# Lists one segment sooner, and GpSimd's fills, an ownership mask, a PSUM bank and a work slot moved, in a segmented attention kernel

## The chip, the cores and the metric

The kernel runs on 1 core of a Trainium2 chip. The metric is the device time of one execution in microseconds (us). Engines: PE (TensorE, matrix products), DVE (VectorE), ACT (ScalarE), POOL (GpSimd, which here also issues the indirect DMAs) and SP (SyncE, which issues most plain DMAs). The core has 16 DMA engines.

## What is computed

```python
N, d = feat.shape                       # 16384, 256; B = 8 segments, LMAX = 3072
q, k, v = feat @ Wq, feat @ Wk, feat @ Wv                       # q, k: 32 columns
starts = jnp.searchsorted(bids, jnp.arange(B)); pos = jnp.arange(N) - starts[bids]
pad = lambda x: jnp.zeros((B, LMAX, x.shape[-1])).at[bids, pos].set(x)
scores = where(mask[:, None, :], einsum('bld,bmd->blm', pad(q), pad(k)), NEG)
rp = einsum('blm,bmd->bld', softmax(scores), pad(v))
t = rp[bids, pos] @ Wt
tn = (t - t.mean(0)) / sqrt(t.var(0) + EPS) * gamma + beta
return feat + relu(tn)
```

The segment numbers `bids` come unsorted, so `pos` of most tokens falls outside 0 to LMAX - 1. Only the tokens that own a slot of a segment take part in its attention (up to 768 a segment on this path). All others read a segment's edge row or nothing.

## The kernel before

Everything is in one function, `fast_path`, which emits for each engine one in-order stream; a small scheduler (`Program`) places the waits. `Wv @ Wt` is folded into one matrix, `wvt`.

- **Lists.** For segment e, `owners(e)` makes the mask of its owners on DVE (seven instructions, up to the running count in `lm[:, e]`). `prefix(lo, hi)` sums counts over partitions by two small PE products into a PSUM bank, and DVE copies them out. `list_tests(e)` writes `ge`, two comparisons of `it16` with the counts, on DVE. `list_half(e, h, bank)` issues six small PE products of `ge` and `lm`; its `finish` turns them on DVE into `idx`, the tokens' numbers, and has GpSimd gather their rows of `feat` into `xs`, three tiles of 128 rows for each half. There are nine lists: 0 to 7 for the segments (up to six tiles), and list 8 (NB) for the repeated rows, tokens that lose their slot to another (up to three tiles, one half, gathered late into `xl` and `tl`).
- **Attention.** Segment e has up to six strips u of 128 query rows. For strip (e, u): `attend` sums PE products over the tiles into PSUM bank `ps_o[u % 2]`; `attended` has DVE take the reciprocal (`rdens`) and ACT write the scaled strip to `tk`, which frees the bank. Beside it the next segment is prepared: `xt_main`, `xt_rest` (turned rows), `project` (q, k), `values` (vs), `scores` (pa, pb). These share two banks `ps_m`, taken in turn by `nb()`; `ps_s[0..3]` hold the scores and, in between, list products. ACT's `square` and DVE's `moments` add up `acc`, the sums for mean and variance.
- **Slots.** Work not tied to a strip waits in a queue, `work`; `slot()` runs one piece of it on DVE: `everyone` (ownership of segments 4 to 7 and list 8), `third` (list 3's ownership, sums and tests), `tables` (row numbers), `one_hot` (matrices `hot`, from rows `eb` that SP loads). `steps` says at which strips of segments 0 to 3 a slot runs.
- **Order of the lists.** In the loop over e, list e + 2 is made at the start of segment e (list 7 in segment 5, list 8 in segment 6), and the tests of list e + 3 at strip 4 of segment e.
- **Fills.** GpSimd's `set` calls clear buffers: a first run at the start, and one behind the gathers of lists 0 and 1: `acc`, `xl`, `tl`, `ridl`, `ecat` and the 16 numbers `turn_of`.
- **The last stage.** After segment 7 the statistics give a scale and a shift. The 16 output groups of 1024 rows (1 MB each) are loaded from `feat` into nine buffers `fb` by `group_in(i)` on SP's queue, DVE or ACT adds the edge rows, and SP stores them. `rows(e)` normalizes the strips in `tk` on DVE, and GpSimd writes them to their rows by 41 indirect DMAs, each segment's behind the store of the last group that it touches. The first buffer `fb[0]` lies over `lm`, `ge`, `it16` and `pos`, so `group_in(0)` has to come behind the last list; it is called at strip (6, 1), and `group_in(1)` at (6, 3).

```python
        ahead = e + 2
        LTs = FT if ahead < NB else LT
        for u in range(FT):
            if ahead <= NB and u == 0 and e:
                first = list_half(ahead, 0, ps_s[2])
            attend(e, u)
            ...
            slot(int(u in steps.get(e, range(FT))))
            if u == 4 and e + 3 <= NB and e:
                list_tests(e + 3, FT if e + 3 < NB else LT)
```

Of the kernel before, what the change touches and what calls it, by code (L numbers as in the profile page):

```python
# [899 lines left out]
def fast_path(nc, feat, bids, wq, wk, wv, wt, gamma, beta, out, bad):  # L900
# [231 lines left out]
    pg.set("POOL", ones_n[:], 1.0 / N)  # L1132
    pg.set("POOL", rdens[:], 1.0)
    pg.set("POOL", graw[:], 0.0)
    for i in range(4):
        s = slice(32 * i, 32 * i + NB)
        pg.dma("SP", graw[s, 0, :], gamma.rearrange("(c i) -> c i", i=32))
        pg.dma("SP", graw[s, 1, :], beta.rearrange("(c i) -> c i", i=32))
# [311 lines left out]
    xt_rest(0, sB)  # L1450
    h1()
    last_()
    pg.set("POOL", acc[:], 0.0)
    pg.set("POOL", xl[:], 0.0)
    pg.set("POOL", tl[:], 0.0)
    pg.set("POOL", ridl[:], NB * FW)
    pg.set("POOL", ecat[:], 0.0)
    for i, g in enumerate(ORDER):
        pg.set("POOL", turn_of[:, g : g + 1], float(i + 1))
    values(0, 0, bank[1])  # L1460
    scores(0, 0, range(4))
    project(0, 1, ps_m[0])
# [22 lines left out]
    def everyone():  # L1485
        def a():
            pg.tt(m3[:], over_e(b_f[:]), over_j(ecol[:]), ALU.is_equal)

        def b():
            pg.tt(w3[:], m3[:], over_j(st_bc[:]), ALU.mult)  # L1490

        def c():
            by_token(pos[:], w3[:])
            pg.tt(pos[:], tok[:], pos[:], ALU.subtract)

        def d():
            pg.ts(below[:], pos[:], -float(LMAX), ALU.is_lt)
            pg.ts(above[:], pos[:], float(LMAX), ALU.is_ge)
            pg.ts(neg[:], pos[:], 0.0, ALU.is_lt)
            pg.tt(lose[:], neg[:], below[:], ALU.subtract)  # L1500
            pg.tt(lose[:], lose[:], same[:], ALU.mult)
            pg.tt(own[:], below[:], above[:], ALU.add)
            pg.tt(own[:], own[:], lose[:], ALU.add)
            pg.ts(own[:], own[:], -1.0, ALU.mult, 1.0, ALU.add)

        def f():
            pg.tt(o3[:], m3[:], over_e(own[:]), ALU.mult)
            for e in range(4, NB):
                pg.scan(lm[:, e, 0:J], ones[:], o3[:, e, :])
            pg.scan(lm[:, NB, 0:J], ones[:], lose[:])  # L1510

        def g():
            for go in prefix(4, NL, ps_s[3]):
                go()

        def g2():
            def by_e(x):
                return x.unsqueeze(2).to_broadcast([1, NB, NG])

            def by_g(x):  # L1520
                return x.unsqueeze(1).to_broadcast([1, NB, NG])

            pg.ts(g16[:], irow[0:1, 0:NG], float(GT * P), ALU.mult)
            pg.tt(gcmp[:], by_e(st_hi[0:1, :]), by_g(g16[:]), ALU.is_gt)
            pg.ts(g16[:], g16[:], float(GT * P), ALU.add)
            pg.tt(gcmp2[:], by_g(g16[:]), by_e(st_lo[0:1, :]), ALU.is_gt)
            pg.tt(gcmp[:], gcmp[:], gcmp2[:], ALU.mult)
            pg.tt(gcmp[:], gcmp[:], by_g(turn_of[:]), ALU.mult)
            pg.red(grp[:], gcmp[:], ALU.max)
            pg.ts(upto[:], grp[:], 1.0, ALU.max)  # L1530
            pg.red(lastg[:], grp[:], ALU.max)
            pg.ts(lastg[:], lastg[:], 1, ALU.max)
            pg.ts(third_l[:], n_bc[0:1, NB:NL], float((LT - 1) * P), ALU.is_gt)
            pg.copy("DVE", armf[:], tiles_i[:])
            pg.red(grp[:, 0:1], armf[:])
            pg.tt(grp[:, 0:1], grp[:, 0:1], third_l[:], ALU.add)
            pg.ts(writes[:], grp[:, 0:1], float(4 * NB + LT - 1), ALU.add, 16.0, ALU.mult)
            pg.ts(over[:, 0:NB], n_bc[:, 0:NB], float(FW), ALU.is_ge)
            pg.ts(over[:, NB:NL], n_bc[:, NB:NL], float(LW), ALU.is_ge)

        def h():
            pg.copy("DVE", br_f[:], br_i[:])
            pg.tt(reads[:], br_f[:], b_f[:], ALU.is_equal)
            pg.stt(reads[:], pos[:], 0.0, reads[:], ALU.is_ge, ALU.mult)
            pg.tt(reads[:], reads[:], own[:], ALU.add)
            pg.dma("SP", reads_of.rearrange("(p j) x -> p (j x)", j=J), reads[:])

        return [a, b, c, d, f, g, h, g2]
# [129 lines left out]
    reads_at = {(NB - 4, 2 + t): (NB - 2, (t,)) for t in range(4)}  # L1678
    reads_at.update({(NB - 3, t): (NB - 2, (3 + t,)) for t in (1, 2)})
    reads_at.update({(NB - 3, 3 + t): (NB - 1, (2 * t, 2 * t + 1)) for t in range(3)})  # L1680
    lag, ready = [], []
    steps = {0: (1, 2, 3, 4, 5), 1: (0, 1, 2, 4, 5), 2: (0, 2, 3, 5), 3: (0, 1, 2, 3, 5)}
    def third():
        owners(3)
        first, then, last_ = prefix(3, 4, ps_s[3])
        first()
        then()
        last_()
        list_tests(3, FT)
# [3 lines left out]
    for e in range(NB - 1):  # L1693
        n = e + 1
        for eng in ("PE", "ACT", "DVE"):
            pg.register(eng, n, tiles_i[0:1, n : n + 1], 2)
        if e == 1:
            todo, choose = tables()
            work.extend(todo)
        if e == 2:  # L1700
            work.extend(one_hot())
            work.append(choose)
        ahead = e + 2
        LTs = FT if ahead < NB else LT
        for u in range(FT):
            if ahead <= NB and u == 0 and e:
                first = list_half(ahead, 0, ps_s[2])
            attend(e, u)
            if e == 0 and u == 0:
                second_list()  # L1710
                attended(e, u)
                first = list_half(ahead, 0, ps_s[2])
            if ahead <= NB and u == 0:
                first()
                if LTs == FT:
                    second = list_half(ahead, 1, ps_s[3])
            slot(int(u in steps.get(e, range(FT))))
            if u == 4 and e + 3 <= NB and e:
                list_tests(e + 3, FT if e + 3 < NB else LT)
            if u == 4:  # L1720
                values(n, 0)
            if u == 5:
                values(n, 1)
            if e == NB - 2 and u == 3:
                group_in(1)
            if (e, u) != (0, 0):
                opened = attended(e, u)
            if u == 0:
                if ahead <= NB and LTs == FT:
                    second()  # L1730
                if ahead == NB:
                    others()
                xt_main(n, 0)
                xt_main(n, 1)
            if u == 1:
                xt_rest(n)
                project(n, 0)
                scores(e, 1, None)
            if u == 3:
                project(n, 1)  # L1740
                scores(n, 0, range(4))
            if u == 4:
                scores(n, 0, range(4, 6))
            if u == 5:
                values(n, 2)
            for x in ready:
                moments(*x)
            ready = []
            lag.append((e, u))
            for _ in range(0 if e == 0 else 2 if u % 2 else 1):  # L1750
                if lag:
                    square(*lag[0])
                    ready.append(lag.pop(0))
            if e == 0 and u == 1:
                pg.tr32(gb[:].rearrange("p s i -> p (s i)"), graw[:].rearrange("p s i -> p (s i)"))
                for e_ in range(3, NB):
                    pg.dma(
                        "SP", xs[:, e_ * FT : (e_ + 1) * FT, :], zt[:].unsqueeze(1).to_broadcast([P, FT, D]), [opened]
                    )
            if e == 0 and u in (1, 5):  # L1760
                pg.copy("ACT", spot[:], ones[:, 0:1])
            if (e, u) in reads_at:
                gather_reads(*reads_at[e, u], opened)
            if e == NB - 2 and u == 1:
                group_in(0)
            if e == NB - 2 and u > 3:
                group_in(u - 2)
            if e == NB - 2 and u == 5:
                group_in(4)
            if e == 4 and u == 3:  # L1770
                pg.set("POOL", tk[:, TT - 2 : TT, :], 0.0)
                pg.register("POOL", "writes", writes[:], 16 * (6 * NB + LT), 16 * (4 * NB + LT - 1))
                pg.register("POOL", "lastg", lastg[:], NG, 1)
                pg.register("POOL", "third", third_l[:], 1)
                for e_ in range(NB):
                    pg.register("POOL", ("g", e_), upto[0:1, e_ : e_ + 1], NG, 1)
                    pg.register("POOL", e_, tiles_i[0:1, e_ : e_ + 1], 2)
# [238 lines left out]
```

## Time and profile before

| | |
|---|---|
| time, median of 3 runs | 312.52 us (310.84 to 314.01) |
| the profiled execution's own time | 313.69 us, of which the span is 311.4 us |
| busy in the span | PE 252.2 us (81%), DVE 229.3 (74%), ACT 135.8 (44%), POOL 129.7 (42%) |
| DMA | 56.82 MB, mean 182 GB/s |
| chain that ended last | PE 39%, DVE 30%, DMA 14%, ACT 7%, issue 6%, POOL 2% |
| mean granted clock of PE | 0.906 |

In a row of a timeline stand the start in us, the duration, the engine, the source line (often that of a helper that records the operation), the operation, what it writes and reads, the shape, a count, and in square brackets how long the engine had been idle and what ended that. A fp32 product shows as two PE instructions.

### The profile page before, as it was taken

The numbers are of one execution on the slowest core, as the hardware profiler recorded it, in microseconds if no ns is written. First come the engines' busy times: TensorE is split into PE (matmuls) and PEld (weight loads), VectorE is DVE, ScalarE is ACT, GpSimd is POOL, SyncE is SP. The second block draws the span as 40 slices with busy tenths as digits, with TensorE's granted clock in tenths as the row PEclk, the third lists the DMA queues.
The fourth block names the chain that finished last, engine by engine and source line by source line (L and its number), as shares of the span: only waits on it lengthen the run. The fifth ranks groups of instructions, "written<-read, shape, count | busy, mean of one in ns | idle before, by whom it ended". The sixth has DMA issues, their size and how long they took to land.

```text
span 311.4 us, 4481 instructions
## 1 busy us (share of the span) xinstructions
PE 252.2 (81%) x1194; PEld 166.8 (54%) x1194; DVE 229.3 (74%) x718; ACT 135.8 (44%) x292; POOL 129.7 (42%) x155
## 2 busy tenths in 40 slices
PE   1779689899799898999999999989977786573820
PEld 1656555766575677687878778757523221121200
DVE  7866788779999896736664765767389999999600
ACT  7346234258474628644754583564421121211110
POOL 3436580340350071006312853742212347778674
PEclk9989796999999999999999999999998579859575
DMA  3102069422122021112021320579999999999984
GB/s 98 35 24 67 3 203 346 157 82 69 52 84 71 34 70 29 67 61 80 27 95 36 90 94 24 196 259 378 339 364 408 349 421 413 402 419 393 424 358 177
DMA packets 23240, 56.82 MB, mean 182 GB/s; under 512 B 4768, under 2 KB 15858, under 8 KB 19114
## 3 DMA queue, kind: packets, MB, share of 16 engines
q1 hardware_dynamic: 17434, 45.77, 39.2%
q0 software_dynamic: 5232, 10.18, 10.2%
q10 hardware_dynamic: 544, 0.52, 0.5%
q8 instruction: 13, 0.21, 0.3%
q14 instruction: 17, 0.14, 0.1%
HBM read 26.73 MB, written 28.61 MB: 178 GB/s over the span
## 4 chain that ended last, share of the span: by engine, by line
PE 39%; DVE 30%; DMA 14%; ACT 7%; issue 6%; POOL 2%; DVEq 1%; SPq 0%; POOLq 0%; ACTq 0%
PE ps L807 37%; DMA out<-f 14%; DVE acc L846 4%; DVE f L826 3%; DVE w L826 2%; DVE junk L833 2%; PE ps L812 2%; DVE k L823 2%; DVE tk L826 2%; POOL out L892 2%; ACT pa L817 1%; DVE ge L835 1%; ACT xT L817 1%; ACT tk L817 1%; DVE both L851 1%
## 5 line engine op out<-in xcount | busy, mean ns | idle before, releaser
L882 POOL DMA_INDIRECT xs<-in_r_feat,idx x48 | 51.0, 1063 | 101.2 <-DVE idx L846 77.1
L807 PE MATMUL ps<-vs,pa 128*128 128x257 f32 x312 | 73.6, 384 | 4.7 <-ACT sq L817 3.6
L807 PEld LDWEIGHTS ps<-vs,pa 128*128 128x128 f32 x312 | 57.1, 189 | 16.5 <-ACT sq L817 4.8
L807 PE MATMUL ps<-f,ident 128*128 128x512 f32 x52 | 38.3, 855 | 19.6 <-DMA f<-in_r_feat 14.4
L892 POOL DMA_INDIRECT out<-tk,idx x39 | 42.9, 1100 | 26.8 <-DVE tk L826 10.4
L817 ACT ACTIVATE tk<-ps,rdens 128x256 f32<-128x256 f32 x46 | 22.2, 483 | 61.8 <-DVE rdens L859 61.8
L807 PE MATMUL ps<-wvt,xT 128*128 128x256 f32 x156 | 39.6, 405 | 0.3 <-ACT pa L817 0.3
L822 ACT COPY f<-ps 128x512 f32<-128x512 f32 x26 | 13.9, 590 | 58.9 <-PE ps L807 58.9
L807 PEld LDWEIGHTS ps<-wvt,xT 128*128 128x128 f32 x156 | 30.9, 202 | 11.0 <-issue 4.3
L807 PEld LDWEIGHTS ps<-f,ident 128*128 128x128 f32 x52 | 11.7, 259 | 36.5 <-DMA f<-in_r_feat 19.3
L846 DVE SCALAR_TENSOR_TENSOR acc<-sq,reads_r,acc 128x256 f32<-128x256 f32 x45 | 21.6, 480 | 8.8 <-ACT sq L817 8.8
L817 ACT ACTIVATE pa<-ps,mask 128x512 f32<-128x512 f32 x39 | 24.0, 690 | 7.5 <-PE ps L807 7.4
L826 DVE TENSOR_TENSOR tk<-tk,ps 128x1024 f32<-128x1024 f32 (+1 forms) x30 | 24.2, 843 | 0.3
L882 POOL DMA_INDIRECT reads_r<-reads_of,idx x12 | 13.4, 1120 | 24.8 <-ACT sq L817 11.8
L826 DVE TENSOR_TENSOR f<-f,ps 128x512 f32<-128x512 f32 x38 | 23.3, 681 | 0.6 <-PE ps L807 0.6
L807 PE MATMUL ps<-q,k 32*128 32x512 f32 (+2 forms) x154 | 21.2, 486 | 1.5 <-ACT pa L817 1.1
L846 DVE SCALAR_TENSOR_TENSOR acc<-tk,reads_r,acc 128x256 f32<-128x256 f32 x45 | 21.5, 478 | 1.2 <-ACT tk L817 0.7
L807 PE MATMUL ps<-xT,w 128*128 128x512 f32 (+1 forms) x60 | 20.5, 474 | 0.5 <-ACT xT L817 0.4
L823 DVE COPY k<-ps 32x128 f32<-32x128 f32 x40 | 11.8, 294 | 12.0 <-PE ps L807 11.1
L807 PE MATMUL ps<-vs,pb 128*128 128x257 f32 x82 | 19.6, 387 | 0.0
L807 PEld LDWEIGHTS ps<-vs,pb 128*128 128x128 f32 x82 | 15.0, 189 | 6.5 <-issue 2.3
L817 ACT ACTIVATE q<-ps,cqk 96x512 f32<-96x512 f32 (+3 forms) x24 | 14.6, 608 | 7.3 <-PE ps L807 7.0
(260 smaller groups left out, 357.1 us busy)
## 6 DMA issues: line engine op xcount, KB each, us to landing
f<-in_r_feat SPq DMA_DIRECT2D x16, 1024.0 KB, 12.8
out<-f SPq DMA_DIRECT2D x16, 1024.0 KB, 15.8
t_rows<-tk SPq DMA_DIRECT2D x8, 512.0 KB, 3.9
xs<-zt SPq DMA_DIRECT2D x5, 768.0 KB, 10.3
t_rows<-tk SPq DMA_DIRECT2D x8, 256.0 KB, 2.2
eb<-edge_of SPq DMA_DIRECT2D x16, 96.0 KB, 2.3
xs<-in_r_feat,idx POOLq DMA_INDIRECT x48, 2.8
out<-tk,idx POOLq DMA_INDIRECT x39, 7.2
```

The costliest lines, as they stand in the source:

```text
L807: "PE", lambda e: e.matmul(out, lhsT, rhs, start=start, stop=stop, skip_group_check=True),
L812: return self.op("PE", lambda e: e.transpose(out, in_, ident), [in_, ident], [out])
L817: "ACT", lambda e: e.activation(out, in_, func, bias=bias, scale=scale), [in_, *more], [out]
L822: return self.op("ACT", lambda e: e.copy(out, in_), [in_], [out])
L823: return self.op(eng, lambda e: e.tensor_copy(out, in_), [in_], [out])
L826: return self.op(eng, lambda e: e.tensor_tensor(out, a, b, op), [a, b], [out])
L833: lambda e: e.tensor_scalar(out, a, s1, s2, op0, op1, accum_out=accum)
L835: else e.tensor_scalar(out, a, s1, s2, op0, op1),
L846: else e.scalar_tensor_tensor(out, a, s, b, op0, op1),
L851: return self.op("DVE", lambda e: e.tensor_reduce(out, in_, AX.X, op), [in_], [out])
L882: lambda e: e.indirect_dma_start(out=out, out_offset=None, in_=table, in_offset=bass.IndirectOffsetOnAxis(ap=ind, axis=0), bounds_check=n ...
L892: lambda e: e.indirect_dma_start(out=table, out_offset=bass.IndirectOffsetOnAxis(ap=ind, axis=0), in_=src, in_offset=None, bounds_check=n ...
```

## The change

- GpSimd's fill of `acc` goes to the first run of fills; the others, as `later_sets`, to the end of strip (1, 0), behind the gathers of list 3.
- `owners(3)` leaves `third` and is called in strip (0, 0), between the second list's tests and its halves.
- `prefix(4, NL)` takes a bank by `nb()` instead of `ps_s[3]`.
- The slot of strip (1, 5) runs behind `attended` instead of ahead of it.
- List 7 is made in segment 4: tests at strip 1, both halves at strip 2 in the `nb()` banks. List 8's tests go to strip 4 of segment 4, its half to the start of segment 5; `others()`, which uses it, stays in segment 6.
- `group_in(0)` is called at strip (5, 1).

```diff
@@ fills
     pg.set("POOL", graw[:], 0.0)
+    pg.set("POOL", acc[:], 0.0)
 ...
-    pg.set("POOL", acc[:], 0.0)
-    pg.set("POOL", xl[:], 0.0)
-    pg.set("POOL", tl[:], 0.0)
-    pg.set("POOL", ridl[:], NB * FW)
-    pg.set("POOL", ecat[:], 0.0)
-    for i, g in enumerate(ORDER):
-        pg.set("POOL", turn_of[:, g : g + 1], float(i + 1))
+    def later_sets():
+        pg.set("POOL", xl[:], 0.0)
        ...
@@ everyone, g
-            for go in prefix(4, NL, ps_s[3]):
+            for go in prefix(4, NL):
@@ the loop over the segments
+    LATE = ((1, 5),)
     def third():
-        owners(3)
 ...
-        ahead = e + 2
+        ahead = e + 2 if e < 5 else NB if e == 5 else NL
 ...
                 second_list()
                 attended(e, u)
+                owners(3)
                 first = list_half(ahead, 0, ps_s[2])
 ...
-            slot(int(u in steps.get(e, range(FT))))
-            if u == 4 and e + 3 <= NB and e:
-                list_tests(e + 3, FT if e + 3 < NB else LT)
+            if e == NB - 4 and u == 1:
+                list_tests(NB - 1, FT)
+            if e == NB - 4 and u == 2:
+                halves = [list_half(NB - 1, h, nb()) for h in range(2)]
+                for go in halves:
+                    go()
+            if (e, u) not in LATE:
+                slot(int(u in steps.get(e, range(FT))))
+            if u == 4 and e in (1, 2, 3, 4):
+                list_tests(e + 3 if e < 4 else NB, FT if e < 4 else LT)
 ...
                 opened = attended(e, u)
+            if (e, u) in LATE:
+                slot()
 ...
-                if ahead == NB:
+                if e == NB - 2:
                     others()
 ...
+            if e == 1 and u == 0:
+                later_sets()
 ...
-            if e == NB - 2 and u == 1:
+            if e == NB - 3 and u == 1:
                 group_in(0)
```

More of the change, by code (lines that the diff above doesn't have):

```diff
@@ L1452, in fast_path @@
     last_()
-    pg.set("POOL", acc[:], 0.0)
-    pg.set("POOL", xl[:], 0.0)
-    pg.set("POOL", tl[:], 0.0)
-    pg.set("POOL", ridl[:], NB * FW)
-    pg.set("POOL", ecat[:], 0.0)
-    for i, g in enumerate(ORDER):
-        pg.set("POOL", turn_of[:, g : g + 1], float(i + 1))
+    def later_sets():
+        pg.set("POOL", xl[:], 0.0)
+        pg.set("POOL", tl[:], 0.0)
+        pg.set("POOL", ridl[:], NB * FW)
+        pg.set("POOL", ecat[:], 0.0)
+        for i, g in enumerate(ORDER):
+            pg.set("POOL", turn_of[:, g : g + 1], float(i + 1))
     values(0, 0, bank[1])
```

## The prediction

> **What bounds the kernel now.** I read the page's slices first, to find the stages, then the table of windows, one row for each stage, then the timelines of the engines where an engine has holes.
>
> ```profile
> core 0: us, PE busy (x) PEld busy (x) DVE busy (x) ACT busy (x) POOL busy (x), PEclk, DMA share, GB/s
> 57.00:122.00 65.00, 59.02 (x316) 43.18 (x314) 58.53 (x200) 36.88 (x89) 19.24 (x18) 1.00 0.22 66
> 122.00:194.00 72.00, 71.14 (x392) 55.60 (x392) 42.93 (x145) 40.67 (x94) 25.06 (x23) 1.00 0.20 62
> 206.00:230.00 24.00, 20.53 (x75) 12.95 (x73) 13.76 (x46) 11.77 (x28) 5.60 (x6) 1.00 0.98 360
> 230.00:294.00 64.00, 43.15 (x165) 14.68 (x166) 62.05 (x92) 12.23 (x24) 38.00 (x34) 0.76 0.99 397
> ```
>
> Four stages with different owners. Ahead of 57 us, as rows further down show, PE and DVE wait for each other in turn and PE's clock drops. From 57 to 122 DVE (58.53 of 65) and PE (59.02) are both nearly full. From 122 to 194 it is PE, 71.14 of 72. From 206 on the DMA engines are full (0.98, 0.99), and between 230 and 294 DVE is nearly full too, 62.05 of 64. So time is to be had in the first stage, where an engine waits, and in the last, where bytes can be taken out; work that only moves inside the two middle stages gives little.
>
> **The change part by part.** *The fills leave segment 0.* They run beside list 2's two tests on DVE:
>
> ```profile
> 33.07 1.60 DVE L835 TENSOR_SCALAR ge<-it,cbeg 128x768 bf16<-128x768 f16 x1
> 34.60 0.76 DVE L835 TENSOR_SCALAR ge<-it,cend 128x768 bf16<-128x768 f16 x1
> 48.08 0.40 DVE L835 TENSOR_SCALAR ge<-it,cbeg 128x768 bf16<-128x768 f16 x1
> 33.69 0.75 POOL L865 MEMSET tl<- 128x768 f32 x1
> 34.73 0.29 PE L807 MATMUL ps<-lm,ge 128*128 128x131 bf16 x1 [2.16 <-DVE ge L835]
> ```
>
> The same test takes 0.40 us at 48.08, with nothing on GpSimd. Here the first ends only behind the fill of tl (33.69 + 0.75 = 34.44, the test 34.67), and the second meets the next fill. So they cost 1.60 + 0.76 - 2 x 0.40 = 1.56, and PE stands idle for 2.16 meanwhile: **-1.6 us**. At least 0, at most 1.6.
>
> *owners(3) moves from the fourth strip of segment 0 into the first.*
>
> ```profile
> 41.85 1.22 DVE L823 COPY k<-ps 32x128 f32<-32x128 f32 x4 [1.19 <-PE ps L807]
> 44.53 0.21 DVE L835 TENSOR_SCALAR own<-b_f 128x128 f32<-128x128 f32 x1
> 46.94 0.18 PE L807 MATMUL ps<-lm,tri 128*128 128x1 bf16 x1 [1.65 <-DVE lm L855]
> 47.48 2.15 PE L807 MATMUL ps<-q,k 32*128 32x512 f32 x8 [0.34 <-issue]
> 54.24 0.17 DVE L859 RECIPROCAL rdens<-ps 128x1 f32<-128x1 f32 x1 [0.84 <-PE ps L807]
> 56.40 0.16 DVE L826 TENSOR_TENSOR lr<-rcol,ps 128x3 f32<-128x3 f32 x1 [1.99 <-PE ps L807]
> ```
>
> Its seven instructions begin at 44.53, and PE's prefix product, which waits 1.65 us for the last of them, starts at 46.94: 2.4 us. PE then waits 0.34 more. With the ownership known earlier, PE goes from its attention strips straight to the scores: **-2.0**. The 2.4 us now stand ahead of list 2's finish on DVE. Behind them wait that list's gathers, a segment before their use, and the reciprocal of the second strip; DVE was about to idle for 1.19 (41.85), so that reciprocal comes some 2.4 - 1.6 = 0.8 later, which the strip already running on PE hides. What is late next is DVE itself: between the two moments it has 1.19 + 0.84 + 1.99 = 4.0 us of idle time, so owners and clock together give 0 to -4.0.
>
> The clock hangs on the same holes:
>
> ```profile
> 31.23:34.64 3.41, 1.34 (x9) 0.94 (x7) 1.99 (x6) 0.19 (x1) 3.10 (x7) 1.00 0.03 3
> 34.64:38.06 3.42, 2.94 (x19) 2.75 (x20) 3.21 (x22) 0.84 (x2) 1.10 (x18) 0.50 0.00 0
> 44.88:48.30 3.42, 1.43 (x11) 0.71 (x11) 2.92 (x15) 0.24 (x1) 1.49 (x2) 1.00 1.05 345
> 48.30:55.12 6.82, 6.82 (x18) 4.48 (x14) 5.09 (x18) 3.75 (x7) 0.00 (x0) 0.50 1.10 342
> ```
>
> Both stretches in which PE was busy for less than half (1.34 of 3.41, 1.43 of 3.42) are followed by a granted clock of 0.50; the second costs 6.82 / 2 = 3.4 us of PE time. With the holes closed, some of it stays at 1.00; DVE lets at most 4.0 - 2.0 = 2.0 of it through. I take the middle, **-1.0**. The Trainium skill, "TensorE: Matmul & The Clock Gate", Part 1, gives the half clock to a whole idle window of about 3.4 us; by that rule the holes of 2 us would not matter, and the sum below would be 1.0 higher. The rows differ: they show the half clock behind windows that were not idle.
>
> *acc's fill* goes to GpSimd's opening run, ahead of its first gather, whose row (the second below) gives GpSimd's wait as 8.15 us: 0, hidden by that wait; at most a fill's length, 0.54, if it held DVE. *The other fills* go behind list 3's gathers:
>
> ```profile
> 82.59 1.15 POOL L882 DMA_INDIRECT xs<-in_r_feat,idx  x1 [15.62 <-DVE idx L846]
> 11.28 1.20 POOL L882 DMA_INDIRECT xs<-in_r_feat,idx  x1 [8.15 <-DVE junk L833]
> 156.87 0.54 POOL L865 MEMSET tk<- 128x512 f32 x1
> 156.89 0.48 DVE L846 SCALAR_TENSOR_TENSOR acc<-tk,reads_r,acc 128x256 f32<-128x256 f32 x1
> 159.75 0.46 DVE L846 SCALAR_TENSOR_TENSOR acc<-tk,reads_r,acc 128x256 f32<-128x256 f32 x1
> ```
>
> GpSimd idles 15.62 us there, so the gathers of list 4 lose nothing. But DVE is the bound there. Beside a fill the moment update with two inputs takes 0.48, without one 0.46: not held. A test or a cast there (br_f is cast in this stretch) may be held like the two tests. Between 0 and twice what the fills cost in the old place, 3.2, I take **+0.7**, one fill's 0.75, the nearest row. The Trainium skill, "GPSIMD Engine Reference", Key points, speaks against this: it names contention with VectorE instructions in a two-port mode *or with two SBUF inputs*. For the first part the trace agrees (1.60 against 0.40), for the second it does not (0.48 against 0.46); by the rule's second part the sum would be 2.0 higher, a rival below.
>
> *The bank of prefix(4..) and the slot of strip (1,5).*
>
> ```profile
> 62.63 0.18 PE L807 MATMUL ps<-lm,tri 128*128 128x5 bf16 x1 [1.50 <-DVE idx L846]
> 79.40 0.47 ACT L817 ACTIVATE tk<-ps,rdens 128x256 f32<-128x256 f32 x1 [1.36 <-DVE rdens L859]
> 80.72 1.14 PE L807 MATMUL ps<-vs,pa 128*128 128x257 f32 x4 [1.92 <-ACT sq L817]
> ```
>
> PE waits 1.50 for list 3's finish to give up bank ps_s[3]. In the new bank it waits for ACT's xT instead, and the next projection, which takes that bank in turn, waits until DVE has read the sums, behind the same finish: 0, within -1.5 and +1.5. At (1,5) the reciprocal no longer stands behind a 1.22 us product, so ACT's 1.36 and most of PE's 1.92 go; but DVE, which has the same work in another order, is full: **-0.3**, within 0 and -1.4.
>
> *The lists.* Per half list PE issues six products and DVE eight instructions with their accumulator reads:
>
> ```profile
> 167.94 0.51 PE L807 MATMUL ps<-lm,ge 128*128 128x131 bf16 x6
> 168.49 0.16 DVE L826 TENSOR_TENSOR lr<-rcol,ps 128x3 f32<-128x3 f32 x1 [1.28 <-PE ps L807]
> 170.01 0.16 DVE L846 SCALAR_TENSOR_TENSOR idx<-ps,jc 128x3 int32<-128x3 f32 x1
> 151.73 0.17 DVE L859 RECIPROCAL rdens<-ps 128x1 f32<-128x1 f32 x1 [0.72 <-PE ps L807]
> 152.74 0.55 ACT L817 ACTIVATE tk<-ps,rdens 128x256 f32<-128x256 f32 x1
> 156.19 2.87 PE L807 MATMUL ps<-vs,pb 128*128 128x257 f32 x12
> ```
>
> Segment 4 gains list 7: 2 x 0.51 on PE. Segment 5 swaps two halves for list 8's one (-0.51), segment 6 loses that (-0.51): PE's sum is 0. DVE gets 2 x 1.7 (168.49 to 170.17) and 1.0 for the tests in segment 4, ahead of the strip's reciprocal at 151.73, which comes near 156.6; ACT's tk follows near 157.1, and PE wants that bank in the strip now at 156.19, then at 157.2. That just holds; I book **+0.5**, within -0.5 and the 11 of rival (d). The gathers of list 7, six at some 1.3 us on GpSimd, go ahead of the small read gathers, which had slack.
>
> *The first group's load* goes from 197 to some 172, where the DMA engines are at 0.20:
>
> ```profile
> f<-in_r_feat SPq DMA_DIRECT2D x16, 1024.0 KB, 12.8
> 197.16 0.42 SPq L877 DMA_DIRECT2D f<-in_r_feat  x1
> SPq L1893 <- DMA out<-f: 47.6, 14, 10.0
> 295.09 0.98 POOL L892 DMA_INDIRECT out<-tk,idx  x1 [1.74 <-SPq L1893]
> 297.66 1.07 ACT L822 COPY f<-ps 128x512 f32<-128x512 f32 x2 [3.10 <-PE ps L807]
> ```
>
> One of 16 loads of 1 MB leaves a stage that moves 397 GB/s: 1.05 MB / 397 = 2.6. SP waits 47.6 us there for stores to land, and GpSimd's last ten writes wait for SP. But the last copies, at 297.66, are paced by DVE's adds and would not move; only what is queued behind them lands earlier: **-1.8**, within 0 and -2.6. On SP the load stands behind the one-hot loads and ahead of two t_rows stores, which had slack.
>
> Sum: -1.6 - 2.0 - 1.0 + 0.7 - 0.3 + 0.5 - 1.8 = **-5.5 us**. Against the profiled execution (313.69, of which 311.4 is span) that is 308.2. The median of the runs shown is 312.52, 1.17 lower, so I predict **307.0**.
>
> **The rivals.** (a) *The clock stays up*: no half-clock stretch before 57 us, all of DVE's idle time used (-1.0 more), the cast not held (-0.7), the load's full 2.6 (-0.8): 304.5. For it: both low stretches follow a hole that goes. Against: windows fall differently from run to run. (b) *The load is hidden anyway*, because DVE paces the last stage (62.05 of 64), or because SP does not come to it before segment 6, so that the change does not do what it says: 307.0 + 1.8 = 308.8. (c) *The fills only move*: each DVE instruction beside them is held (+2.0), and the clock falls as now (+1.0): 310.0. For it: they now stand in a stage that DVE bounds; against, the update at 156.89. (d) *Slower*: in segment 4 list 7's two finishes hold the strip's reciprocal back past 157.2, so PE waits for its bank, in the stage in which PE is the bound. DVE's lag is 4.9 us (151.73 to 156.6), and at 42.93 of 72 busy it takes some 12 us to work off: three to four windows of 3.41. A window with 2 us of hole costs these and 1.7 by the half clock behind it; three cost 11.1, so -6.0 + 11.1 = +5.1, 317.6. It decides from holes of 2 us in a window on.
>
> **How the numbers follow.** Forecast 0.38, (a) 0.18, (b) 0.15, (c) 0.20, (d) 0.09. A change within 1% (309.4 to 315.6) is about what a measurement of this kernel can't tell from none, its three runs spreading from 310.84 to 314.01. Faster by more than that: nearly all of the forecast and (a), three quarters of (b), a fifth of (c): 0.70. Slower: 0.09. The rest, 0.21, lies within. The range goes from 302.4, (a) with the bounds of the slot (-1.1 more) and of the lists (-1.0), to 311.8, (c) with the load hidden as well (+1.8); it leaves out (d) and some of (c).
>
> **What would show it.** Right: tests of list 2 at 0.40 us each; no wait of PE for lm before the scores of segment 1; list 3's first finish, now at 56.40, near 52; a granted clock of 1.00 where 48.30 to 55.12 has 0.50; list 7's gathers near 149 and the first group's load near 168; no new waits of PE for ACT's tk in segment 4; the last copies, now at 297.66, near 294, and the end some 1.8 nearer to them. Wrong: DVE instructions of several times their length behind list 3's gathers; half-clock slices after 100 us; the last copies early, but the end not.

## The result: 2.1 us faster where 5.5 were forecast, and the profile after

The changed kernel takes 310.43 us (median of 21 runs, 306.95 to 312.13) against 312.52 for the kernel before (median of 21 runs, 309.65 to 314.35): 2.1 us less, or 0.9933 of it. The ratios given here and below are of the fast runs alone, without those more than 1.5% above the fastest of the same kernel: 0.9916, 95% interval 0.989 to 0.9943, or 2.6 us. By either figure that is faster, by less than the 1% that I called a measurable difference and by less than half of the forecast. The profiled execution of the changed kernel took 307.55 us (span 305.2). That looks like the forecast, but is the fourth shortest of its 21 runs.

What the forecast named is there. The table of windows and the timelines of the changed kernel:

```profile
31.00:34.41 3.41, 2.21 (x25) 1.95 (x24) 3.03 (x18) 0.90 (x2) 1.00 (x1) 1.00 0.02 0
34.41:37.83 3.42, 3.42 (x13) 2.26 (x12) 3.11 (x17) 0.79 (x2) 0.00 (x0) 1.00 0.00 0
54.90:58.31 3.41, 1.54 (x6) 0.80 (x7) 2.57 (x20) 2.41 (x5) 2.44 (x3) 0.99 0.93 302
58.31:61.72 3.41, 3.41 (x7) 1.97 (x6) 1.21 (x5) 2.15 (x4) 2.83 (x4) 0.51 0.36 99
122.00:194.00 72.00, 71.99 (x393) 56.72 (x392) 44.66 (x143) 41.01 (x94) 28.29 (x25) 1.00 0.27 82
226.00:290.00 64.00, 45.51 (x168) 14.93 (x165) 61.90 (x91) 12.79 (x24) 39.18 (x36) 0.74 1.00 399
```

```profile
31.70 0.55 DVE L835 TENSOR_SCALAR ge<-it,cbeg 128x768 bf16<-128x768 f16 x1
32.17 0.40 DVE L835 TENSOR_SCALAR ge<-it,cend 128x768 bf16<-128x768 f16 x1
50.33 0.16 DVE L826 TENSOR_TENSOR lr<-rcol,ps 128x3 f32<-128x3 f32 x1 [1.16 <-issue]
54.77 0.14 DVE L859 RECIPROCAL rdens<-ps 128x1 f32<-128x1 f32 x1
79.75 0.16 DVE L859 RECIPROCAL rdens<-ps 128x1 f32<-128x1 f32 x1
152.05 0.11 DVE L859 RECIPROCAL rdens<-ps 128x1 f32<-128x1 f32 x1
168.61 0.42 SPq L877 DMA_DIRECT2D f<-in_r_feat  x1
290.97 1.07 ACT L822 COPY f<-ps 128x512 f32<-128x512 f32 x2 [2.79 <-PE ps L807]
```

List 2's tests take 0.55 and 0.40 us (1.60 and 0.76 before), list 3's first finish comes at 50.33 instead of 56.40, the first group's load at 168.61 instead of 197.16, and between 122 and 194 PE has no hole (71.99 of 72). New is the half clock at 58.31 to 61.72, behind a window in which PE was busy for 1.54 of 3.41 us.

Both kernels were profiled again, three profiles of before and four of the changed kernel in all. The reciprocals of strips (1, 0) and (2, 0) and DVE's first add mark the stages. The first two rows are starts in us, the others lengths of a stretch in us:

| | before | changed | means moved by |
|---|---|---|---|
| reciprocal of (1, 0) | 60.85, 60.34, 60.92 | 54.77, 56.64, 56.46, 57.70 | -4.3 |
| reciprocal of (2, 0) | 84.05, 83.53, 84.11 | 79.75, 82.77, 82.49, 82.67 | -2.0 |
| from list 2's first test to the reciprocal of (1, 0) | 27.78, 26.83, 26.32 | 23.07, 23.00, 22.90, 22.88 | -4.0 |
| from there to the reciprocal of (2, 0) | 23.20, 23.19, 23.19 | 24.98, 26.13, 26.03, 24.97 | +2.3 |
| from the first add to the end | 80.70, 79.49, 79.84 | 78.84, 79.82, 78.10, 78.80 | -1.1 |

The starts also hold what differs by chance before list 2's tests, which begin at 33.07, 33.51 and 34.60 in before and at 31.70, 33.64, 33.56 and 34.82 in the changed kernel; the stretches don't. So the first stage gained 4.0, nearly what was forecast (1.6 + 2.0 + 1.0 = 4.6), segment 1 took back more than half of it, and the last stage gave less than 1.8.

### The profile page after: what moved, and what is told of

It is laid out like the page before. It is cut to its first block, busy times and chain, and to the rows that moved or that the text cites. A ratio compares the mean times of both kernels' runs of the same rounds, so it can differ in the third digit from the quotient of the medians.

```text
span 305.2 us, 4480 instructions
## 1 busy us (share of the span) xinstructions
PE 248.3 (81%) x1194; PEld 163.3 (54%) x1194; DVE 228.3 (75%) x718; ACT 134.9 (44%) x292; POOL 131.3 (43%) x155
## 4 chain that ended last, share of the span: by engine, by line
PE 37%; DVE 31%; DMA 14%; issue 7%; ACT 6%; POOL 1%; DVEq 1%; POOLq 0%; SPq 0%; ACTq 0%
PE ps L807 35%; DMA out<-f 14%; DVE acc L846 4%; DVE f L826 3%; DVE junk L833 3%; DVE w L826 2%; DVE tk L826 2%; POOL out L892 1%; PE ps L812 1%; ACT pa L817 1%; DVE k L823 1%; DVE ge L835 1%; DVE both L851 1%; ACT pb L817 1%; ACT tk L817 1%
## 5 line engine op out<-in xcount | busy, mean ns | idle before, releaser
L882 POOL DMA_INDIRECT xs<-in_r_feat,idx x48 | 52.3, 1090 | 100.7 <-DVE idx L846 64.4
L807 PE MATMUL ps<-vs,pa 128*128 128x257 f32 x312 | 75.1, 388 | 4.6 <-ACT tk L817 2.2
L807 PE MATMUL ps<-wvt,xT 128*128 128x256 f32 x156 | 37.1, 384 | 0.5 <-DVE acc L846 0.3
L807 PEld LDWEIGHTS ps<-wvt,xT 128*128 128x128 f32 x156 | 28.9, 190 | 9.9 <-issue 3.5
L882 POOL DMA_INDIRECT reads_r<-reads_of,idx x12 | 14.1, 1178 | 20.8 <-ACT sq L817 11.2
L859 DVE RECIPROCAL rdens<-ps 128x1 f32<-128x1 f32 x46 | 7.5, 162 | 13.7 <-PE ps L807 13.6
```

What stands on the lines that cost most here:

```text
L807: "PE", lambda e: e.matmul(out, lhsT, rhs, start=start, stop=stop, skip_group_check=True),
L859: return self.op("DVE", lambda e: e.reciprocal(out, in_), [in_], [out])
L882: lambda e: e.indirect_dma_start(out=out, out_offset=None, in_=table, in_offset=bass.IndirectOffsetOnAxis(ap=ind, axis=0), bounds_check=n ...
```

## Experiment 1: the same two kernels again

No edit; two copies of each.

> The kernel before, unchanged, one more execution, to see what differs from one execution to the next. Theory P (phase): the profiled execution of before was an unlucky one, with two half-clock stretches ahead of 57 us; here the first reciprocal of segment 2, at 84.05 us there, comes 1.5 to 3 us sooner (81 to 82.5), and the last stage (first add at 230.67 to the end at 311.37, 80.7 us) stays within 0.5 us. Theory T (tail): the reciprocal comes at 84 as before, and the last stage is what differs, by 1 to 3 us.

> The changed kernel, unchanged, one more execution. Theory P: the reciprocal of segment 2 stays near 79.75 us, and the last stage (226.39 to 305.23, 78.8 us) within 0.5 us. Theory T: the reciprocal at 79.75, and the last stage 1 to 3 us longer, 80 to 82, with the half-clock stretches of PE in other places of it.

> As before_a, a second sample: Theory P puts the reciprocal of segment 2 at 81 to 82.5 us, Theory T at 84 with a last stage of 79 to 82 us.

> As after_a, a second sample: Theory P puts the last stage at 78.8 us within 0.5, Theory T at 80 to 82 us.

Before, 314.51 and 318.18; changed, 311.55 and 309.61. Theory P fell: before's first profile was typical up to segment 2. Theory T's 84 came in both profiles of before, its 79.75 in neither of the changed kernel's. It was the changed kernel's first profile that was lucky: the gain of some 4 us at (1, 0) is 1.3 to 1.6 at (2, 0) in after_a and after_b, against 4.3 in the first profile. Of the 3.0 us between the first profile and after_a at (2, 0), 1.9 are there at list 2's tests already, and 1.1 come in segment 1: in both repeats the clock is halved over two stretches there, in the first profile over one. The timeline of PE in after_a, then in before_a:

```profile
57.93 0.18 PE L807 MATMUL ps<-lm,tri 128*128 128x5 bf16 x1 [2.14 <-ACT xT L817]
58.59 0.66 PE L812 MATMUL ps<-ident,xs 128*128 128x128 f32 x2 [0.46 <-issue]
59.25 3.78 PE L807 MATMUL ps<-xT,w 128*128 128x512 f32 x4
```

```profile
62.11 0.18 PE L807 MATMUL ps<-lm,tri 128*128 128x5 bf16 x1 [1.50 <-DVE idx L846]
62.34 0.41 PE L812 MATMUL ps<-ident,xs 128*128 128x128 f32 x2
62.65 1.98 PE L807 MATMUL ps<-xT,w 128*128 128x512 f32 x4
```

and the windows of after_a, then of before_a:

```profile
54.81:58.22 3.41, 1.19 (x7) 0.63 (x5) 3.24 (x17) 1.40 (x3) 2.80 (x3) 1.00 1.07 341
58.22:65.05 6.83, 6.46 (x12) 3.57 (x13) 3.11 (x16) 3.79 (x9) 5.59 (x23) 0.50 0.45 141
```

```profile
58.00:61.42 3.42, 2.62 (x16) 2.04 (x14) 3.31 (x14) 0.91 (x2) 2.39 (x3) 1.00 0.22 64
61.42:64.83 3.41, 2.69 (x10) 1.52 (x11) 1.90 (x14) 2.15 (x7) 2.47 (x3) 1.00 0.36 95
```

PE now comes to strip (1, 1) some 4 us sooner, but DVE still has the ownership of segments 4 to 7 ahead of the reciprocal of (1, 0). Behind that reciprocal stand ACT's tk and xT, and in the new bank PE's prefix product waits for xT: 2.14 us, where it waited 1.50 for list 3's finish. This leaves one window with PE busy for only 1.19 of 3.41 us, the clock is halved behind it, and the same projection takes 3.78 instead of 1.98 us. In before the hole lies across two windows (2.62 and 2.69), and the clock stays.

Before's two repeats also lose 2.5 and 4.1 us in segment 5, in a pause of ACT that no semaphore of the program explains (before_a; in before_b the pause is 3.10 us, and the row names a PE product that had ended before it):

```profile
181.67 3.05 ACT L817 ACTIVATE pb<-ps,mask 128x128 f32<-128x128 f32 x11 [3.32 <-remote]
```

No profile of a kernel with the change's first-stage parts shows it, not even the one with the old lists (experiment 2). What it is stays open, and so does how many of the 21 runs of before have it. Before's median differs with the chip as well (312.3 to 316.1 in the experiments below), so each kernel is compared with what ran beside it.

## Experiment 2: one part undone at a time

```diff
# no_fills: acc's fill and later_sets back behind the gathers of list 1
# no_owners
@@ strip (0, 0)
                 attended(e, u)
-                owners(3)
@@ third
+        owners(3)
# no_lists: lists 7 and 8, their tests and group_in(0) in their old segments
# no_load
-            if e == NB - 3 and u == 1:
+            if e == NB - 2 and u == 1:
                 group_in(0)
```

> The changed kernel with GpSimd's fills back behind the gathers of list 1 (acc's too). The prediction: the tests of list 2 take 1.60 and 0.76 us again and 1.6 comes back, 0.7 is saved in segment 1: 0.9 slower than the changed kernel, 311.3 us, 0.995 of before. Rival 1, the fills cost nothing in the new place: 1.6 slower, 312.0, 0.998. Rival 2, the gain of the first stage is lost at 58 to 65 whatever comes before it: no difference beyond 0.5 us, 310.4, 0.992.

> The changed kernel with owners(3) back in the fourth strip of segment 0. The prediction: 2.0 and the clock's 1.0 come back, 313.4 us, 1.003 of before, with PE's wait for lm of 1.65 us and half clock at 48 to 55. Theory H: the hole and the half clock only move back from 58 to 65 to 48 to 55, the reciprocal of (2, 0) is within 1 us of the changed kernel's, and the time 310.4 to 311.4, 0.992 to 0.996.

> The changed kernel with lists 7 and 8 and the first group's load back in their old segments; fills, ownership, bank and slot stay. The prediction: the load's 1.8 comes back, the lists' 0.5 is saved, 1.3 slower than the changed kernel, 311.7 us, 0.997 of before. Theory S (segment 5 of the old order holds a stall of ACT and DVE at 178 to 182, seen in two of three profiles of before and in none of three of the changed kernel): on top of that 2 to 4 us in a profile that has the stall, 312.5 to 314, 1.00 or above.

> The changed kernel with the first group's load back at strip (6, 1); the lists stay sooner. The prediction: 1.8 slower than the changed kernel, 312.2 us, 0.998 of before. Rival (b), DVE's adds pace the last stage (62.9 us from the first to the last in every profile) and the load is hidden anyway: 310.4 us, 0.992.

Beside before at 312.29: no_fills 310.69, 0.997 (0.9923 to 1.0016); no_owners 310.92, 0.9977 (0.9934 to 1.0019); no_lists 309.95, 0.9919 (0.9882 to 0.9956). Against the change's 0.9916, undoing the fills' move costs 0.0054 x 312.5 = 1.7 us and undoing that of the ownership 1.9, each within some 1.7; by the medians it is 0.5 and 0.7. So the times alone don't tell the forecasts of no_fills apart.

The profiles, one of each, show more. From list 2's first test to (1, 0) no_fills takes 25.37 us and no_owners 25.18, where the changed kernel takes 22.9 to 23.1: there the two moves are worth 2.4 and 2.2. From (1, 0) to (2, 0) they take 23.49 and 24.17, where the changed kernel takes 25.0 to 26.1 and before 23.2: in neither is the clock halved between 57 and 66. By (2, 0) the moves are worth only 0.4 and 0.9. In no_owners the clock is halved at 44.2 to 51.1 instead, and at 71.6 to 75.0, which is close to Theory H.

no_fills has the changed kernel's wait for xT, but the hole falls across two windows. The clock stays, and the projection takes its 1.98 us:

```profile
58.06 0.18 PE L807 MATMUL ps<-lm,tri 128*128 128x5 bf16 x1 [2.05 <-ACT xT L817]
59.39 1.98 PE L807 MATMUL ps<-xT,w 128*128 128x512 f32 x4 [0.25 <-DVE n L835]
```

```profile
54.26:57.67 3.41, 1.75 (x9) 1.18 (x7) 3.31 (x12) 0.71 (x2) 2.20 (x3) 1.00 1.09 354
57.67:61.09 3.42, 2.32 (x8) 1.18 (x9) 1.87 (x15) 2.23 (x6) 2.48 (x3) 1.00 0.78 244
```

So the wait by itself costs segment 1 some 0.3 us (23.49 against 23.2). With the half clock behind it the changed kernel loses 1.8 to 2.9.

Undoing the lists and the load together changes nothing that the times show (0.9919 against 0.9916, within some 1.4). In no_lists the marks run even from (2, 0) to (7, 3), 2.4 us ahead of before at both; the changed kernel loses 0.8 in segment 4 (reciprocal at 152.05) and has it back in segments 5 and 6, which have fewer half lists. no_load took 310.14 on a chip where before took 316.11, 0.9846 (0.9779 to 0.9913), without the changed kernel beside it; experiment 4 puts the load beside a twin.

no_fills shows the holding in segment 0 once more (DVE, GpSimd), and that cast of segment 1 free of it:

```profile
31.41 2.52 DVE L835 TENSOR_SCALAR ge<-it,cbeg 128x768 bf16<-128x768 f16 x1
32.93 0.76 POOL L865 MEMSET tl<- 128x768 f32 x1
63.51 0.22 DVE L823 CAST br_f<-br_i 128x128 f32<-128x128 int32 x1
```

## Experiment 3: away with the hole

Three ways: another order on DVE (late10), the same and the prefix product behind the projection (late11), or idle products in the holes (warm).

```diff
# late10
-    LATE = ((1, 5),)
+    LATE = ((1, 0), (1, 5))
# late11: LATE = ((1, 0), (1, 1), (1, 5)), and for u == 1 the slot runs here:
                 project(n, 0)
+                if (e, u) in LATE:
+                    slot()
                 scores(e, 1, None)
# warm: behind attend(1, 1), and the same behind prefix(2, 3)
+                for _ in range(3):
+                    pg.mm(ps_o[1][:, 258:508], ident[:], wvt[:, 0, 0:250])
# late11_warm: late11, and the three behind prefix(2, 3)
```

> The changed kernel, with one more slot moved: that of strip (1, 0), the ownership of segments 4 to 7 on DVE (some 2.9 us), runs behind that strip's reciprocal instead of ahead of it. Theory H (hole): what the changed kernel gains by 57 us it loses again between 58 and 72, because PE's hole from 55.8 to 57.9 (2.1 us, on ACT's xT, which stands behind tk and so behind this reciprocal) puts the half clock on 58 to 65. With the reciprocal ahead, the hole is about 1.2 us, the projections at 59 to 63 take 2.0 us instead of 3.8, the reciprocal of strip (2, 0) comes near 80 instead of 82.6, and the time is 307.5 to 308.5 us, 0.984 of before. Theory D (DVE is the bound there anyway): the same DVE work in another order, the reciprocal of (2, 0) stays at 82.5, the time at 310.4, 0.992 of before.

> The changed kernel with the slots of strips (1, 0) and (1, 1) moved: the ownership of segments 4 to 7 behind the reciprocal of (1, 0), their prefix product behind the first projection of (1, 1), so that PE goes from attend straight to transposes and projection, in the other of the two banks. Theory C: no hole above 0.6 us between 54 and 60, clock 1.00 there, reciprocal of (2, 0) near 79.5 to 80, 307 to 308 us, 0.983 of before. Theory D (DVE paces segment 1 whatever PE's clock): reciprocal of (2, 0) at 82 or later, 310.4 us, 0.992.

> The changed kernel with three idle products of 128 x 250 (some 1.5 us) for PE in each of its two holes of the first stage: behind attend of strip (1, 1), where PE waits 2.1 us for ACT's xT, and behind the prefix product of list 2, where it waits 2.0 us for the tests. No wait is taken away. Theory C (the clock): a stretch of 3.4 us in which PE is busy for less than some 1.6 us brings the half clock on the next; filled, the clock stays at 1.00 from 58 to 65 and from 34 to 38, the reciprocal of strip (2, 0) comes near 80 instead of 82.6, and the time is 307.5 to 308.5 us, 0.985 of before. Theory W (the waits themselves, and DVE's load behind them): the reciprocal of (2, 0) stays at 82 to 83, the time at 310 to 311, 0.992 to 0.994.

> As late11, with the three idle products behind the prefix product of list 2 as well. Theory C: also no half clock at 34 to 38, where three of the changed kernel's and of before's six profiles or more have one: 0.5 to 1 us less than late11 in the median, 306.5 to 307.5 us, 0.981 of before. Theory D: as late11, 310.4 us.

late10: 309.62, 0.9918 (0.9877 to 0.9959), no gain over the change, since the hole only changed its owner. The prefix product waits 1.03 for lm, and then the projection waits 1.65 for DVE to read the sums out of the bank that it needs next:

```profile
55.39 0.17 PE L807 MATMUL ps<-lm,tri 128*128 128x5 bf16 x1 [1.03 <-DVE lr L826]
57.70 3.78 PE L807 MATMUL ps<-xT,w 128*128 128x512 f32 x4 [1.65 <-DVE n L835]
```

warm, late11 and late11_warm, beside before at 316.11: 0.9826 (0.9756 to 0.9897), 0.9858 (0.9782 to 0.9933), 0.9822 (0.9751 to 0.9894); with no_load at 0.9846, none stands out. In warm the clock did stay at 1.00 from 54 to 71, and the reciprocal of (2, 0) came at 81.23, 1.3 to 1.5 sooner than in after_a, after_b and after_c, half of what Theory C said (a halved stretch at 71.5 to 74.9 came on top). What took the rest was in the forecast and hardly in the changed kernel's profiles (0.22 to 0.43): the cast of br_f. DVE and GpSimd in late11, then in warm, and DVE in after_a:

```profile
62.32 2.08 DVE L823 CAST br_f<-br_i 128x128 f32<-128x128 int32 x1
62.87 0.75 POOL L865 MEMSET xl<- 128x768 f32 x1
63.55 0.75 POOL L865 MEMSET tl<- 128x768 f32 x1
```

```profile
62.68 0.75 POOL L865 MEMSET xl<- 128x768 f32 x1
62.90 0.48 DVE L846 SCALAR_TENSOR_TENSOR acc<-sq,reads_r,acc 128x256 f32<-128x256 f32 x1
63.30 1.41 DVE L823 CAST br_f<-br_i 128x128 f32<-128x128 int32 x1
64.07 0.54 POOL L865 MEMSET ecat<- 128x512 f32 x1
```

```profile
65.17 0.22 DVE L823 CAST br_f<-br_i 128x128 f32<-128x128 int32 x1
```

Two losses hide each other. With the clock halved, DVE comes in after_a to the cast at 65.17, when the long fills are over. With the clock up it comes at 62 to 63.5 and is held until a fill has ended: 64.40 in late11, behind the fill of tl (63.55 + 0.75 = 64.30), and 64.71 in warm, behind that of ecat (64.07 + 0.54 = 64.61). That is 1.41 to 2.08 us for an instruction of 0.22. The moment update of two inputs in warm, beside the fill of xl, takes its usual 0.48; the fill's row names no input. The Trainium skill, "GPSIMD Engine Reference", Key points, names contention of GpSimd with VectorE in a two-port mode or with two SBUF inputs; the casts and tests agree with such contention, the update's 0.48 does not show the second part, in the new place as in the old one.

## Experiment 4: both away, and the load by itself

```diff
# cast, and with it warm_cast and late11_cast
@@ everyone, a
+            pg.copy("DVE", br_f[:], br_i[:])
             pg.tt(m3[:], over_e(b_f[:]), over_j(ecol[:]), ALU.is_equal)
@@ everyone, h
-            pg.copy("DVE", br_f[:], br_i[:])
```

> The changed kernel again, beside the next three. Both theories: half clock over one or two stretches of 3.4 us between 57 and 66, the cast of br_f at 0.22 to 0.43 us, reciprocal of strip (2, 0) at 80 to 83; its time is what the other three are compared with.

> The changed kernel with one DVE instruction moved: the cast of br_f (0.22 us alone) goes from strip (1, 2) to segment 0, away from the fills. Theory M (two losses that hide each other): where the clock is halved at 58 to 65, DVE comes to the cast only behind the fills, and the cast costs 0.22 anyway; so no change against the changed kernel, within 0.4 us. Theory F (the fills are the loss): 1.2 to 1.9 us faster than the changed kernel.

> warm (three idle products of PE in each of the two holes) with the cast of br_f in segment 0. Theory M: clock 1.00 at 58 to 65 and nothing held on DVE, the reciprocal of (1, 2) some 5.1 us behind that of (1, 1) as where the fills are in segment 0 (6.3 in warm, 6.9 in the changed kernel), that of (2, 0) near 80, and 1.5 to 2.5 us faster than the changed kernel. Theory D (DVE paces segment 1 anyway): no difference beyond 0.5 us.

> late11 (ownership of segments 4 to 7 behind the reciprocal of (1, 0), its prefix product behind the first projection of (1, 1)) with the cast of br_f in segment 0. In late11 the cast took 2.08 us. Theory M: reciprocal of (2, 0) near 79, 2 to 3.5 us faster than the changed kernel. Theory D: no difference beyond 0.5 us.

Beside before at 312.38: changed 309.46, 0.9893 (0.9839 to 0.9946); cast 309.46, 0.9888 (0.9835 to 0.9941); warm_cast 309.22, 0.9893 (0.9855 to 0.993); late11_cast 308.12, 0.9872 (0.9824 to 0.9921). cast's reciprocal of (2, 0) is at 82.76, after_c's at 82.67, both with the clock halved from 60.7 on, as Theory M says; the times, each within some 1.7, could not tell Theory F's 1.2 from nothing. warm_cast misses, and decides between neither theory: the clock was halved all the same, behind a window of 1.92:

```profile
56.42:59.83 3.41, 1.92 (x10) 1.08 (x9) 3.10 (x22) 1.94 (x4) 2.47 (x3) 1.00 1.04 329
59.83:63.24 3.41, 3.41 (x6) 1.48 (x5) 0.31 (x2) 1.65 (x4) 2.80 (x4) 0.50 0.36 115
```

late11_cast fits Theory M in its profile (reciprocal of (2, 0) at 79.97, 2.7 ahead of after_c, of which 1.1 are there at list 2's tests, 33.74 against 34.82). Its time is only 1.3 ahead, within the noise, where Theory M said 2 to 3.5. It was run again, with a twin that has the load back in segment 6.

> late11_cast again, beside the next one. Theory M: reciprocal of strip (2, 0) at 79 to 81, no half clock between 54 and 70, 0.982 to 0.990 of before, as the first time (0.987). If that first time was luck, 0.99 or above and a half clock in that stretch.

> late11_cast with the first group's load back at strip (6, 1). The prediction's term: 1.8 us slower than late11_cast, in the stretch from DVE's first add to the end. Rival (b), the load is hidden because DVE's adds pace that stage (62.9 us from the first to the last of them in nearly every profile): no difference beyond 0.6 us.

late11_cast_d 310.36, 0.9896 (0.9841 to 0.995); late11_cast_no_load 309.42, 0.9872 (0.9834 to 0.9909). The same program, twice. The timeline of PE and the windows of late11_cast:

```profile
60.47 0.18 PE L807 MATMUL ps<-lm,tri 128*128 128x5 bf16 x1 [2.51 <-ACT q L817]
61.01 3.75 PE L807 MATMUL ps<-vs,pa 128*128 128x257 f32 x16 [0.33 <-issue]
```

```profile
56.40:59.81 3.41, 1.56 (x4) 0.38 (x2) 3.15 (x17) 1.17 (x4) 2.52 (x3) 1.00 1.05 338
59.81:63.23 3.42, 2.43 (x12) 2.08 (x13) 2.45 (x13) 2.00 (x5) 2.81 (x4) 1.00 0.38 118
```

and of late11_cast_d:

```profile
60.58 0.19 PE L807 MATMUL ps<-lm,tri 128*128 128x5 bf16 x1 [2.51 <-issue]
61.12 6.70 PE L807 MATMUL ps<-vs,pa 128*128 128x257 f32 x16 [0.33 <-issue]
```

```profile
56.93:60.34 3.41, 1.14 (x3) 0.19 (x1) 2.83 (x16) 1.58 (x4) 2.53 (x3) 1.00 1.00 321
60.34:67.17 6.83, 6.27 (x16) 4.98 (x17) 4.41 (x18) 2.36 (x6) 4.82 (x23) 0.50 0.23 70
```

Up to 61 us the two differ by 0.11. The same hole of 2.51 us falls across two windows in the first (1.56 and 2.43 busy) and mostly into one in the second (1.14). There the clock is halved for 6.83 us, the 16 products of two strips take 6.70 instead of 3.75, and the reciprocal of (2, 0) comes at 83.05 instead of 79.97. So a halved clock in this place costs 3.0 us beyond those 0.11, and in this pair where the grid of windows falls decides whether it comes. By the forecast of late11_cast_d, a half clock there means that the first time was luck.

With late11 and late11_warm, four profiles of this order show how the losses hide each other. From list 2's first test to the reciprocal of (2, 0) it takes 46.23 us with neither (late11_cast), 47.18 with the cast held (late11, 2.08), 49.18 with the clock halved (late11_cast_d), and 48.93 with both (late11_warm, cast 2.07, profiled in its longest run). By these, one profile each, the held cast costs 0.9 with the clock up and nothing with it halved.

late11 hadn't closed the hole either, only moved it to 58. The Trainium skill, "TensorE: Matmul & The Clock Gate", Part 1, calls the activity window free-running, and this pair agrees. It also asks for a whole idle window, which the rows don't show: windows with 1.14, 1.19 and 1.54 us of work (late11_cast_d, after_a and the changed kernel's first profile) were followed by the half clock. Nor does PE's busy time in the window settle it: windows of 1.56 (late11_cast) and 1.75 us (no_fills) kept the clock, and windows of 1.92 (warm_cast), 2.12 (late11_cast, 18.85 to 22.26) and 2.62 (no_fills, 95.23 to 98.64) lost it. What the clock goes by is left open.

The load: late11_cast and late11_cast_no_load run alike to DVE's first add. That add, the last copies of ACT and GpSimd's last write of each:

```profile
226.66 6.07 DVE L826 TENSOR_TENSOR f<-f,ps 128x512 f32<-128x512 f32 x10 [0.55 <-PE ps L807]
290.03 1.07 ACT L822 COPY f<-ps 128x512 f32<-128x512 f32 x2 [1.87 <-PE ps L807]
300.24 0.99 POOL L892 DMA_INDIRECT out<-tl,idx  x1 [0.30 <-issue]
```

```profile
226.61 6.07 DVE L826 TENSOR_TENSOR f<-f,ps 128x512 f32<-128x512 f32 x10 [0.55 <-PE ps L807]
292.59 1.07 ACT L822 COPY f<-ps 128x512 f32<-128x512 f32 x2 [2.73 <-issue]
301.88 1.00 POOL L892 DMA_INDIRECT out<-tl,idx  x1 [0.30 <-issue]
```

With the early load the last copies come 2.6 sooner, GpSimd's last write 1.6 and the end 1.1 (305.17 against 306.27). The times don't show even that (310.36 with, 309.42 without). From the first add to the last DVE takes 62.9 us in both, as rival (b) said. Over all profiles, the stretch from the first add to the end took 78.0 to 81.7 us with the early load and 78.9, 79.3 and 79.7 with the late one. So the load is worth at most the 1.1 of this pair, and no gain of it is shown.

No version is shown to beat the changed kernel: late11_cast has the lowest median beside it (308.12 against 309.46), and once more 310.36 on another chip.

## Why the forecast was wrong, by its own steps

- **Fills leave segment 0, -1.6, and owners(3), -2.0: right up to (1, 0).** Undone, 2.4 and 2.2 us come back between list 2's tests and (1, 0), and only 0.4 and 0.9 by (2, 0).
- **Clock, -1.0: the step that failed.** The low stretch at 48 to 55 went, as forecast, but in all four profiles of the changed kernel another one came between 57 and 66. I had asked only whether holes *before* 57 close, and had costed the bank at 0 within 1.5 without a halved clock behind it. Its wait (for ACT's xT) I had named, but not that PE, 4 us early, would meet DVE's old order there and that the half clock behind a hole of 2 us costs far more than the wait. Sign and size both: segment 1 took back 2.3 in the mean. It takes 23.2 us in before, 23.5 in no_fills with this wait and the clock up, and 25.0 or 26.1 in the changed kernel with one or two halved stretches, 1.5 to 2.6 more than in no_fills.
- **Fills in the new place, +0.7:** the mechanism was right, cast included, but 0 in the changed kernel (0.22 to 0.43), since the halved clock makes DVE late. With the clock up the cast was held for 0.7 to 1.9 in other orders of the same work (no_owners, warm, late11).
- **Lists, +0.5: 0.** The loss of 0.8 in segment 4 is there and comes back in segments 5 and 6. The reciprocal's lag in segment 4, for which I wrote 4.9 (the terms given, 2 x 1.7 and 1.0, make 4.4), was 4.6, from 4.3 ahead of before to 0.3 behind. Rival (d) did not come: 71.99 of 72.
- **Load, -1.8: mis-sized,** at most 1.1. I let the bytes (2.6) shorten a stretch that DVE's adds set.
- **Slot of (1, 5), -0.3, and the bank, 0,** were not tried by themselves. Whether PE's hole in segment 1 would be there with the old bank is open.
- The sum by what was shown is -4.0 to (1, 0), +2.3 to (2, 0), and 0 to -1.1 in the last stage: -1.7 to -2.8, against -2.1 by the medians and -2.6 by the ratio (0.0084 x 312.5). ACT's pause, in two of the three profiles of before, is not in this sum. The time lands next to rival (c)'s 310.0, of whose two parts one came true: the clock falls as before, only later. That its number is so near is luck, since its other part and the load's 1.8 did not come.

## What to carry to other kernels

A wait that is closed on one engine comes back where that engine next meets the slower one: follow the freed engine until it waits again, and price that wait with what follows it, not by its own length. Where the clock is granted by windows, one profile is a throw of dice of some 3 us here: profile both kernels several times before reading a difference of 1%. Two losses in one place can hide each other, so taking away one may show nothing.

## What was not expected of the hardware

- A cast of 128 x 128 took 0.22 us alone and 0.43, 0.90, 1.41 and 2.08 us beside the same fills (the changed kernel's first profile, no_owners, warm, late11). It ended 0.1 us behind the end of one of them: that of tl in no_owners and late11, that of ecat in the first profile and warm.
- The same program halved its clock or didn't by where a hole of 2.51 us fell on the grid of 3.41 us: 3.0 us of 310. Windows with PE busy for 1.14 to 1.54 us were followed by half clock, those of 1.56 and 1.75 were not, and those of 1.92 (nearly half of it idle products), 2.12 and 2.62 were.
- ACT paused for 3.3 and 3.1 us in segment 5 with nothing of the program to wait for, in two of three profiles of before and in none of the other kernels'.
